# A four-layer graph network on one core: scores from the values' product, row vectors turned on VectorE, and graph attention's loops in step with the attention's half slots

## The chip, the cores and the metric

The kernel runs on one core of a Trainium2 chip. The core has TensorE (PE, matrix products, with weight loads shown apart as PEld), VectorE (DVE), ScalarE (ACT), GpSimd (POOL) and SyncE (SP), whose queue issues nearly all transfers here. The metric is the device time of one launch in microseconds; less is better. The time of the kernel before the change is 4863.75 us, the median of three runs (4861.99 to 4867.91).

## What is computed

Eight samples (B = 8) of N = 2048 nodes with 128 features pass through four layers, each as `x = x + layer(relu(layernorm(x)), adj)`. One 0/1 matrix `adj` (2048 x 2048, symmetric, with its diagonal) is shared. Everything is f32.

```python
def layer0(x):                       # graph attention with a normalised projection
    x = x * node_weights + node_bias + x
    h = layernorm(x @ W) * ln_gamma + ln_beta
    e = leaky_relu((h @ a1)[:, :, None] + (h @ a2)[:, None, :], 0.2)
    p = softmax(where(adj > 0, e, NEG_INF))
    return elu(p @ h + h)

def layer1(x):                       # four heads of 32, masked dot-product attention
    q, k, v = heads(x @ W_q), heads(x @ W_k), heads(x @ W_v)
    p = softmax(where(adj == 0, -inf, q @ k.T / sqrt(32)))
    return merge(p @ v) @ W_o + b_o

def layer2(x):                       # mean over the neighbours
    return relu(x @ W_self + b_self + (mask @ x / deg) @ W_neigh + b_neigh)

def layer3(x):                       # graph attention
    h = x @ W3.T
    e = leaky_relu((h @ a_src)[:, :, None] + (h @ a_dst)[:, None, :], 0.2)
    return softmax(where(adj == 0, -1e9, e)) @ h
```

## The kernel before

**The main stream.** Layer 1's attention is the longest part and is the frame for all else. It is cut into 8 x 8 x 4 = 256 blocks: sample, 256 rows of queries, head. A block has 12 positions (`SUB`), six for each half of 128 rows. In a half, position 0 issues the scores on PE (`scores`, L876) and the exponentials of the half before on ACT (L900); positions 0 and 1 also issue products of an earlier block's values (L927); position 2 masks the scores on DVE (L892); positions 3 and 4 transpose an earlier block's exponentials on PE (L912); positions 4 and 5 copy the transposed tiles to SBUF on ACT (`eT`, L917). A sample has 32 blocks, 384 positions.

**The side stream.** While the attention of sample b runs, the side work is layer 2 and layer 3 of sample b-1, layer 0 of sample b+1 and the projections for its attention, and the first part of layer 0 for sample b+2. It is written as a list of steps (`Steps`), each a few functions with a weight. `merged` lays two lists beside each other by weight. `work` then spreads the functions evenly over the positions of the window by their weights. The order of PE, DVE, ACT and POOL is the order in which this code issues instructions; each of these engines takes its instructions in that order. SP's order comes from the scheduler.

**Graph attention's loop** (`gat_loop`), used by layers 0 and 3. The 16 tiles of rows form six groups of 3, 3, 3, 3, 2, 2. For a group, the loop goes over 8 pairs of column tiles, and each pair passes through stages that lie one step apart:

- `leaky` (L464, ACT): leaky ReLU of the row scores along the free axis (`ab`, first half) plus a column score as bias;
- `lowered` (L470, DVE): minus the row's maximum (`ab`, second half);
- `exps` (L474, ACT), then `masked` (L479, DVE);
- `product` (L490, PE): 2 x n products into `gacc`; then `ended` and `closed`, which divide and add to x.

After the 8 pairs comes one step that starts no pair (`+ [None]`). Beside the pairs of one group, the steps of `ahead` prepare the next: the masks' load (`mg`), the maxima over a row's neighbours (`gat_maximum`, L404, DVE, with a load of `pmg`; in layer 0 all 16 are done before the loop), then `shifts` and `spread` in the fourth and fifth steps.

**Row vectors.** `spread` and `gat_rows` need vectors that lie along partitions turned along the free axis and copied to all partitions. `along_free` does it: a transpose on PE into PSUM (`prow`, L360), a copy on DVE put off by `later` (L364), a write to a small DRAM tile (`rowd`, L366), and a read that broadcasts it (`ab` or `s2b`, L367).

**Scores.** Layer 0 multiplies by W (L352), copies the result to `haug` (L561), normalises it (stats, root, apply, then gamma and beta on POOL, L567 and L570), turns it on PE again (`turned2`, copied by ACT as `h0nT`, L342) and multiplies the turned chunk with the two halves of `a` (`gat_scores`, L383). Layer 3 multiplies the turned chunk twice: with W3 transposed (L352) and with `wa3`, which is W3 transposed times the halves of `a` (L383). DVE copies the results to `s1` and `s2` and scales `s2n` (L386 to L388).

**PSUM.** The main and the side stream share three buffers of two banks (`ps2`). `later` keeps a read of such a buffer back until the next step or until a buffer is needed (`settle`, `psum`).

Of the kernel before, what the change touches and what calls it, by code (L numbers as in the profile page):

```python
# [18 lines left out]
P = 128  # L19
# [12 lines left out]
def gnn_kernel(  # L32
# [143 lines left out]
    nc.gpsimd.memset(neg_half, -0.5)  # L176

# [10 lines left out]
    w0 = load_w("w0", W0)  # L188
# [16 lines left out]
    NR = 2 * T + 4  # L205
# [4 lines left out]
    nc.scalar.dma_start(out=rows[2 * T + 2 : NR], in_=a3.rearrange("(c f) o -> c (f o)", c=2))  # L210
# [8 lines left out]
    a12_3 = cols[:, 2 * T + 2 : NR]  # L219
    w3T = const.tile([P, P], F32, name="w3T")  # L220
    pw3 = psum("pw3", (P, P))
    nc.tensor.transpose(pw3, w3, ident)
    nc.vector.tensor_copy(w3T, pw3)

    wa3 = const.tile([P, 2], F32, name="wa3")
    pwa = psum("pwa", (P, 2))
    nc.tensor.matmul(pwa, w3, a12_3, start=True, stop=True)
    nc.vector.tensor_copy(wa3, pwa)
# [12 lines left out]


# [44 lines left out]
    def norm_stages(src, dst, relu=False):  # L287
# [44 lines left out]

        return [stats, root, shift, apply_relu] if relu else [stats, root, apply]
# [14 lines left out]
    def rows_times(srcT, w, name):  # L348

        pt = psum(name)  # L350
        for k in range(4):
            nc.tensor.matmul(pt[:, k, :], srcT[:, k * P : (k + 1) * P], w, start=True, stop=True)  # L352
        return pt

    def along_free(col, dst):


        n = col.shape[1]
        pt = psum("prow", (n, P))
        nc.tensor.transpose(pt, col, ident)  # L360

        def read():
            row = small("row", (T, P))[0:n, :]
            nc.vector.tensor_copy(row, pt)  # L364
            d = new(dr2, "rowd", "rowd", (T, P))
            nc.sync.dma_start(out=d[0:n, :], in_=row)  # L366
            nc.sync.dma_start(  # L367
                out=dst, in_=d[0:n, :].rearrange("t p -> (t p)").partition_broadcast(P)
            )

        later(read)


    def gat_scores(st, g, hT, a12):

        if g == 0:
            st["s1"] = small("s1", (P, T))
            st["s2"] = small("s2", (P, T))
            st["s2n"] = small("s2n", (P, T))
        c = slice(4 * g, 4 * g + 4)  # L380
        pc = psum("psc", (P, 4, 2))
        for k in range(4):
            nc.tensor.matmul(pc[:, k, :], hT[:, k * P : (k + 1) * P], a12, start=True, stop=True)  # L383

        def read():
            nc.vector.tensor_copy(st["s1"][:, c], pc[:, :, 0])  # L386
            nc.vector.tensor_copy(st["s2"][:, c], pc[:, :, 1])
            nc.vector.tensor_scalar(st["s2n"][:, c], st["s2"][:, c], -1.0 / UP, None, ALU.mult)  # L388

        later(read)  # L390

    def gat_rows(st):

        st["s2b"] = new(sp2, "s2b", "s2b", (P, N))
        along_free(st["s2n"], st["s2b"])
# [12 lines left out]
    def gat_loop(st, finish, maxima):  # L408
# [19 lines left out]

        def shifts(k):
# [4 lines left out]
            cab = small("cab", (P, 6))[:, 0 : 2 * n]  # L434
# [4 lines left out]
        def spread(k):  # L439
            n = GROUPS[k][1]  # L440
            t = new(abp, "ab", "ab", (P, 2 * n * P))
            along_free(gr[k]["cab"], t)
            gr[k]["s1"], gr[k]["m"] = t[:, 0 : n * P], t[:, n * P : 2 * n * P]

        def ahead(k):
            if k >= len(GROUPS):
                return []
            return [
                [lambda: fetch(k), lambda: maximum(k, 0)],
                [lambda: fetch_mask(k, 0), lambda: maximum(k, 1)],  # L450
                [lambda: maximum(k, 2)],
# [65 lines left out]
        for k in range(len(GROUPS)):  # L517
            items += [(k, jp) for jp in range(T // 2)] + [None]
        stages = [leaky, lowered, exps, masked, product, ended, closed]
        nxt = []  # L520
        for step in range(len(items) + len(stages) - 1):
# [7 lines left out]
            for s in reversed(range(len(stages))):  # L529
                if 0 <= step - s < len(items) and items[step - s]:  # L530
                    fns.append(lambda f=stages[s], a=items[step - s]: f(*a))
# [4 lines left out]
    def layer0_ahead(b):  # L536

        st, h, hT, h2T = {}, {}, {}, {}
# [17 lines left out]
        def project(g):  # L556
# [4 lines left out]
            later(lambda: nc.scalar.copy(st["haug"][:, 4 * g : 4 * g + 4, 0:P], pt))  # L561
# [10 lines left out]
        def turned2(g):  # L572
            h2T[g] = chunk("h0nT")
            turn(hv(g), h2T[g])
# [7 lines left out]
            + norm_stages(hv, hv)  # L582
            + [scale, shift, turned2, lambda g: gat_scores(st, g, h2T.pop(g), a12_0)],
# [11 lines left out]
    def layer0_loop(b, st, maxima=False):  # L595
# [21 lines left out]
        return gat_loop(st, finish, maxima)  # L617
# [3 lines left out]
    def before_attention(b):  # L621
# [19 lines left out]
        def project(g):  # L641
            pq = psum("pq", (P, 512))
            nc.tensor.matmul(pq, wq, hT[g], start=True, stop=True)

            def read_q():
                qs = chunk("qs")
                nc.scalar.activation(qs, pq, AF.Copy, scale=-1.0 / (math.sqrt(HD) * UP))
                nc.sync.dma_start(out=qd[g], in_=qs)

            later(read_q)  # L650
            pk = psum("pk", (P, 512))
            nc.tensor.matmul(pk, wk, hT[g], start=True, stop=True)

            def read_k():
                kc = chunk("kc")
                nc.scalar.copy(kc, pk)
                nc.sync.dma_start(out=kd[g], in_=kc)

            later(read_k)
# [131 lines left out]
    def layer3(b):  # L791
# [13 lines left out]
        def project(g):  # L805
# [3 lines left out]
            pt = rows_times(hT[g], w3T, "ph3")  # L809
            later(lambda: nc.scalar.copy(st["haug"][:, 4 * g : 4 * g + 4, 0:P], pt))  # L810
# [5 lines left out]
            + [turned, project, lambda g: gat_scores(st, g, hT.pop(g), wa3)],  # L816
            1.0,
        )
        pre.add(1.0, lambda: gat_rows(st))
# [16 lines left out]
        return pre, gat_loop(st, finish, True)  # L836
# [245 lines left out]
    def mask_steps():  # L1082
# [35 lines left out]
        def degrees():  # L1118
# [10 lines left out]
            row = small("row", (T, P))  # L1129
# [32 lines left out]
    with tc.manual_schedule(engines=ENGINES):  # L1162
# [17 lines left out]
        LAG = 2 * SUB + 14  # L1180
# [26 lines left out]

        sts = {}
        for b in range(B):
            side = Steps()  # L1210
            if b >= 1:
                pre2, agg = layer2(b - 1)
                side.extend(pre2)
                pre3, loop3 = layer3(b - 1)
# [90 lines left out]
```

## Time and profile before

The profiled execution took 4871.3 us, and its span, from the first instruction to the last, is 4869.5 us. The page gives the busy time of each engine over the span, and groups of instructions with how often they ran, the busy time, the mean duration in ns, and the idle time of the engine just before them with what ended it. "out<-in" are the names of the tiles.

| what | value |
|---|---|
| median of three runs | 4863.75 us |
| profiled execution, its span | 4871.3 us, 4869.5 us |
| mean granted TensorE clock | 0.946 of full speed |
| ACT `eT` copies, L917 | 1024, busy 1018.4 us |
| ACT exponentials of the attention, L900 | 512, busy 1027.8 us |
| DVE masking of the attention, L892 | 1024, busy 1211.3 us |
| PE transposes of the attention, L912 | 8192 records, busy 1098.5 us |
| PE products of graph attention, L490 | 8192 records, busy 1114.1 us |
| ACT and DVE of graph attention, L464, L474, L470, L479 | 800.6, 591.5, 666.4, 662.0 us |
| DVE maxima, L404 | 256, busy 584.7 us |
| ACT `leaky` waiting for the transfer of `ab` | 96.3 us in 17 waits, the longest 22.3 |
| DVE waiting for `psc` (L386) | 90.4 us in 35 waits |

A row of the table is read so: the busy time is the sum of what the engine spent on the group, not of what the kernel would be shorter without it.

### The profile page before, as it was taken

How to read it: one execution, taken by the hardware profiler on the slowest of the kernel's cores; microseconds unless marked ns; L12 is line 12 of the kernel's file. 1: busy time of each engine (PE TensorE's matmuls, PEld its weight loads, DVE VectorE, ACT ScalarE, POOL GpSimd, SP SyncE). 2: the span in 40 equal slices, each digit the busy share in tenths (PEclk: the TensorE clock that was granted, in tenths of full speed). 3: DMA queues.
4: the chain of work that ended last, by engine and by line, in shares of the span. 5: the costliest groups of instructions: out<-in, count | busy, mean ns of one | idle time of the engine just before them, and what ended most of it. 6: DMA issues, size and time to landing. Idle time of an engine off the chain costs nothing.

```text
span 4869.5 us, 88275 instructions
## 1 busy us (share of the span) xinstructions
PE 4236.4 (87%) x34037; PEld 2898.0 (60%) x34037; DVE 3863.5 (79%) x8268; ACT 3643.9 (75%) x5153; POOL 437.4 (9%) x407
## 2 busy tenths in 40 slices
PE   3668998898998889898898988988899988999976
PEld 3545655565656666475665656566565656656645
DVE  5957776788978888788987889788887888758849
ACT  4637986697858888497885978588884888848926
POOL 2020002001200021001200012000210000000000
PEclk7868999999999999999999999999999999999988
DMA  8421123213231132312333132421324113222122
GB/s 269 135 88 54 47 61 97 92 49 102 81 126 57 57 107 79 124 50 76 91 105 95 57 94 85 122 65 55 107 76 130 48 58 98 79 86 62 47 92 75
DMA packets 303741, 423.37 MB, mean 87 GB/s; under 512 B 55844, under 2 KB 173016, under 8 KB 299224
## 3 DMA queue, kind: packets, MB, share of 16 engines
q1 hardware_dynamic: 301376, 416.84, 28.2%
q8 instruction: 269, 4.41, 0.4%
q14 instruction: 152, 1.25, 0.1%
q10 hardware_dynamic: 1944, 0.87, 0.1%
HBM read 365.77 MB, written 55.98 MB: 87 GB/s over the span
## 4 chain that ended last, share of the span: by engine, by line
PE 40%; DVE 31%; ACT 21%; issue 4%; DMA 4%; SPq 0%; POOL 0%; ACTq 0%; DVEq 0%; POOLq 0%
DVE e L892 9%; PE gacc L490 9%; PE pt L912 9%; ACT eT L917 6%; ACT e L900 6%; PE pagg L737 6%; PE sc L876 5%; DVE dump L404 5%; DVE ge L479 4%; DVE ge L470 4%; PE acc L927 4%; ACT ge L464 4%; ACT ge L474 2%; DVE ln_s L297 1%; DMA ab<-rowd 1%
## 5 line engine op out<-in xcount | busy, mean ns | idle before, releaser
L917 ACT COPY eT<-pt 128x1024 f32<-128x1024 f32 x1024 | 1018.4, 1011 | 666.4 <-PE pt L912 663.2
L892 DVE CUSTOM_DVE_ANT_0 e<-sc,pm 128x1024 f32<-128x1024 f32 x1024 | 1211.3, 1220 | 214.7 <-PE sc L876 205.6
L912 PE MATMUL pt<-ident,e 128*128 128x128 f32 x8192 | 1098.5, 282 | 187.0 <-DVE amh L892 106.0
L490 PE MATMUL gacc<-haug,ge 128*128 128x129 f32 x8192 | 1114.1, 286 | 123.4 <-DVE ge L479 121.2
L490 PEld LDWEIGHTS gacc<-haug,ge 128*128 128x128 f32 x8192 | 1011.9, 198 | 264.4 <-issue 134.7
L912 PEld LDWEIGHTS pt<-ident,e 128*128 128x128 f32 x8192 | 940.2, 145 | 341.4 <-DVE amh L892 137.4
L900 ACT ACTIVATE e<-e,amn 128x2048 f32<-128x2048 f32 x512 | 1027.8, 2007 | 20.9 <-DVE amn L896 20.8
L464 ACT ACTIVATE ge<-ab,s 128x384 f32<-128x384 f32 (+1 forms) x1536 | 800.6, 574 | 96.6 <-DMA ab<-rowd 96.3
L876 PE MATMUL sc<-ks,qr 32*128 32x512 f32 x4096 | 765.2, 668 | 55.8 <-ACT eT L917 40.5
L470 DVE TENSOR_TENSOR ge<-ge,ab 128x768 f32<-128x768 f32 (+1 forms) x768 | 666.4, 869 | 112.5 <-ACT ge L464 107.6
L479 DVE SCALAR_TENSOR_TENSOR ge<-mg,ge 128x768 f32<-128x768 fp8e4 (+1 forms) x768 | 662.0, 863 | 87.3 <-ACT ge L474 85.2
L474 ACT ACTIVATE ge<-ge 128x768 f32<-128x768 f32 (+1 forms) x768 | 591.5, 772 | 78.4 <-DVE ge L470 75.0
L927 PE MATMUL acc<-eT,vv 128*32 128x256 f32 x8192 | 612.5, 400 | 3.9 <-ACT eT L917 3.8
L404 DVE CUSTOM_DVE_ANT_0 dump<-s2b,pmg 128x2048 bf16<-128x2048 f32 x256 | 584.7, 2284 | 28.4 <-DMA s2b<-rowd 23.8
L307 POOL TENSOR_TENSOR ln_r<-ln_ve,neg_half 128x4 f32<-128x4 f32 x160 | 224.9, 1405 | 3872.8 <-DVE ln_ve L301 3781.0
L927 PEld LDWEIGHTS acc<-eT,vv 128*32 128x32 f32 x8192 | 196.6, 111 | 509.1 <-issue 430.2
L876 PEld LDWEIGHTS sc<-ks,qr 32*128 32x128 f32 x4096 | 231.9, 190 | 230.7 <-ACT eT L917 120.5
L737 PE MATMUL pagg<-mt,hm 128*128 128x512 fp8e4 x1536 | 356.7, 381 | 7.9 <-DVE agT L755 7.9
L737 PEld LDWEIGHTS <-hm 128*128 128x128 bf16 x1536 | 147.2, 98 | 182.0 <-issue 30.2
L339 PE MATMUL ptr<-ident,h 128*128 128x128 f32 x512 | 93.1, 308 | 46.1 <-DVE h L314 16.6
L980 DVE TENSOR_TENSOR aoT<-po,rT 128x256 f32<-128x256 f32 x64 | 27.1, 424 | 125.0 <-ACT rT L975 125.0
L339 PEld LDWEIGHTS ptr<-ident,h 128*128 128x128 f32 x512 | 65.5, 154 | 87.2 <-issue 26.6
(120 smaller groups left out, 2779.4 us busy)
## 6 DMA issues: line engine op xcount, KB each, us to landing
pmg<-pm_all SPq DMA_DIRECT2D x256, 256.0 KB
mg<-mg_all SPq DMA_DIRECT2D x128, 384.0 KB
pm<-pm_all SPq DMA_DIRECT2D x128, 256.0 KB
qr<-qd SPq DMA_DIRECT2D x1024, 32.0 KB
mt<-mt_all SPq DMA_DIRECT2D x64, 512.0 KB
ab<-rowd SPq DMA_DIRECT2D x64, 384.0 KB
adj<-in_adj_dram SPq DMA_DIRECT2D x16, 1024.0 KB
s2b<-rowd SPq DMA_DIRECT2D x16, 1024.0 KB
```

The costliest lines, as they stand in the source:

```text
L404: nc.vector.tensor_tensor_reduce(dump, st["s2b"], pm, UP, HIGHEST, ALU.add, ALU.min, st["mn"][:, it : it + 1])
L464: nc.scalar.activation(e[:, c, :], gr[k]["s1"], AF.Prelu, bias=st["s2"][:, j : j + 1], alpha=ALPHA)
L470: nc.vector.tensor_tensor(e, e, bc_mid(gr[k]["m"], 2), ALU.subtract)
L479: nc.vector.scalar_tensor_tensor(e, mt, BIG, e, ALU.mult, ALU.min)
L490: nc.tensor.matmul(gr[k]["acc"][:, q, :], e[:, c, q * P : (q + 1) * P], st["haug"][:, j, :], start=(j == 0 and q == 0), stop=(j == T - 1), ...
L737: nc.tensor.matmul(st["pa"], st["hm"][:, j, s, :], st["mt", g, j // 8][:, j % 8, :], start=(j == 0 and s == 0), stop=(j == T - 1 and s == ...
L876: nc.tensor.matmul(blk["sc"][g // 2][:, (g % 2) * 512 : (g % 2 + 1) * 512], blk["q"][r, t * P : (t + 1) * P], ks_t[b, hh][r, :], start=Tru ...
L892: nc.vector.tensor_tensor_reduce(e[:, c], blk["sc"][h], pm[:, c], UP, HIGHEST, ALU.add, ALU.min, mh[:, h : h + 1])
L900: nc.scalar.activation(blk["e"][t], blk["e"][t], AF.Exp, scale=-1.0, bias=blk["mn"][:, t : t + 1], accum_out=blk["ao"]["sum"][:, t, blk["h ...
L912: nc.tensor.transpose(pt[:, c, t, :], blk["e"][t][:, j * P : (j + 1) * P], ident)
L917: nc.scalar.copy(eT, blk.pop(("pt", w)).rearrange("p c t n -> p c (t n)"))
L927: nc.tensor.matmul(pair["acc"][g * HD : (g + 1) * HD, blk["hh"] % 2, :], vv_t[blk["b"], blk["hh"]][:, j, :], blk["eT"][w][:, g, :], start= ...
```

## The change

**Scores as further columns.** `w0` and `w3T` become 130 columns wide. The last two columns of `w3T` hold W3 transposed times the halves of `a`; those of `w0` hold W times gamma times the halves of `a`. `rows_times` then gives, beside the 128 values, the two scores of each node in the same products. In layer 0 they belong to the values before normalisation, so `gat_scores` corrects them with the mean, the inverse deviation and two sums per half (`gab`), in five small DVE instructions after a copy out of PSUM (`zs`). The second turn, its ACT copy and the products of `gat_scores` go. Layer 0's `score` stage stands after the root of the variance and before `apply`.

**Row vectors on DVE.** `along_free` turns with `nc.vector.transpose`, in 32 x 32 blocks. The vectors lie in zeroed tiles of 32 columns (`cabs`, three in turn; `s2ns`, two). The turned row then lies in four pieces on four groups of partitions, so four transfers write it to DRAM, and one broadcasts it as before. The transpose and its transfers are issued at once, not put off.

**q and k** of a chunk share one PSUM tile (`pqk`), read by one put-off function.

**Loops in step.** For samples 1 to 6, `work` now covers only layer 2, the maxima of layer 0 and the first five steps of layer 0's loop, in 63 positions. Then `locked` issues one loop step for every three positions (half of the six positions of a half of a block): each function of the step stands behind the first, second or third of them as `PLACES` (positions 0 to 2 of a half) or `PLACES_B` (positions 3 to 5) say. The steps of layer 3's preparation, or of the attention's preparation, are spread over the loop's first 0.7 or 0.6. In these windows the step without a pair after each group goes (`gap` is 0), and the five opening steps of layer 3's loop lie beside the last steps of layer 0's loop. `LAG`, by which the side stream ends after the window, is 36 positions and was 38.

```diff
     def rows_times(srcT, w, name):
-        pt = psum(name)
+        n = w.shape[1]
+        pt = psum(name, (P, 4, P if n == P else 2 * P))
         for k in range(4):
-            nc.tensor.matmul(pt[:, k, :], srcT[:, k * P : (k + 1) * P], w, start=True, stop=True)
+            nc.tensor.matmul(pt[:, k, 0:n], srcT[:, k * P : (k + 1) * P], w, start=True, stop=True)
         return pt
 
-    def along_free(col, dst):
-        n = col.shape[1]
-        pt = psum("prow", (n, P))
-        nc.tensor.transpose(pt, col, ident)
-        def read():
-            row = small("row", (T, P))[0:n, :]
-            nc.vector.tensor_copy(row, pt)
-            d = new(dr2, "rowd", "rowd", (T, P))
-            nc.sync.dma_start(out=d[0:n, :], in_=row)
+    def along_free(col, dst, n):
+        row = small("row", (P, 32))
+        nc.vector.transpose(row, col)
+        d = new(dr2, "rowd", "rowd", (T, P))
+        for g in range(4):
             nc.sync.dma_start(
-                out=dst, in_=d[0:n, :].rearrange("t p -> (t p)").partition_broadcast(P)
+                out=d[0:n, g * 32 : (g + 1) * 32], in_=row[g * 32 : g * 32 + n, :]
             )
-        later(read)
+        nc.sync.dma_start(
+            out=dst, in_=d[0:n, :].rearrange("t p -> (t p)").partition_broadcast(P)
+        )
 
-    def gat_scores(st, g, hT, a12):
+    def gat_scores(st, g, src, mean=None, r=None):
...
-        pc = psum("psc", (P, 4, 2))
-        for k in range(4):
-            nc.tensor.matmul(pc[:, k, :], hT[:, k * P : (k + 1) * P], a12, start=True, stop=True)
-        def read():
-            nc.vector.tensor_copy(st["s1"][:, c], pc[:, :, 0])
-            nc.vector.tensor_copy(st["s2"][:, c], pc[:, :, 1])
-            nc.vector.tensor_scalar(st["s2n"][:, c], st["s2"][:, c], -1.0 / UP, None, ALU.mult)
-        later(read)
+        s = st["s"][:, 4 * g : 4 * g + 4, :]
+        if mean is None:
+            nc.vector.tensor_copy(s, src)
+        else:
+            for c in range(2):
+                nc.vector.scalar_tensor_tensor(
+                    src[:, :, c], mean, gab[:, c : c + 1], src[:, :, c], ALU.mult, ALU.subtract
+                )
+            nc.vector.tensor_tensor(src, src, bc_last(r, 2), ALU.mult)
+            nc.vector.scalar_tensor_tensor(
+                s, src, -1.0, bc_mid(gab[:, 2:4], 4), ALU.mult, ALU.add
+            )
+        nc.vector.tensor_scalar(
+            st["s2n"][:, 4 * g : 4 * g + 4], s[:, :, 1], -1.0 / UP, None, ALU.mult
+        )
...
-            items += [(k, jp) for jp in range(T // 2)] + [None]
+            items += [(k, jp) for jp in range(T // 2)] + [None] * gap
...
+        PLACES = {'product': 1, 'masked': 0, 'exps': 1, 'lowered': 0, 'leaky': 1, 'ended': 1, 'closed': 0, 'maxi': 0, 'other': 2}
+        PLACES_B = {'product': 1, 'masked': 0, 'exps': 0, 'lowered': 1, 'leaky': 0, 'ended': 1, 'closed': 1, 'maxi': 1, 'other': 2}
+
+        def locked(loop, other, share):
+            k = 0
+            for n, (_, fns) in enumerate(loop):
+                cell = [[], [], []]
+                pl = PLACES_B if pos[0] % 6 >= 3 else PLACES
+                for f in fns:
+                    cell[pl[getattr(f, "place", "other")]].append((f, False))
+                want = min(len(other), math.ceil(len(other) * (n + 1) / (len(loop) * share)))
+                parts = []
+                while k < want:
+                    parts += [(f, i == 0) for i, f in enumerate(other[k][1])]
+                    k += 1
+                for i, p in enumerate(parts):
+                    cell[(i * 3) // len(parts)].append(p)
+                for c in cell:
+                    mains[pos[0]]()
+                    pos[0] += 1
+                    for f, first in c:
+                        if first:
+                            settle()
+                        f()
...
-                loop0 = layer0_loop(b + 1, sts[b + 1])
-                side.extend(merged(loop0, pre3, 0.85) if pre3 else loop0)
+                loop0 = layer0_loop(b + 1, sts[b + 1], gap=int(b == 0))
                 tail = before_attention(b + 1)
...
                 if loop3:
-                    side.extend(merged(loop3, tail, 0.7))
-                else:
-                    side.extend(tail)
+                    end = (b + 1) * per + LAG
+                    side.extend(loop0[:5])
+                    both = loop0[5:-6]
+                    both += [(0.0, u[1] + v[1]) for u, v in zip(loop0[-6:-1], loop3[:5])]
+                    both += [(0.0, loop0[-1][1] + loop3[5][1])] + loop3[6:]
+                    n = len(loop0) - 6
+                    work(side, end - 3 * len(both))
+                    locked(both[:n], pre3, 0.7)
+                    locked(both[n:], tail, 0.6)
+                    continue
+                side.extend(loop0)
+                side.extend(tail)
```

## The prediction

> **What bounds the kernel now.** I read the page's first part first, then the chain of waits, then the busy time of each engine by stretch.
>
> ```profile
> PE 4236.4 (87%) x34037; PEld 2898.0 (60%) x34037; DVE 3863.5 (79%) x8268; ACT 3643.9 (75%) x5153; POOL 437.4 (9%) x407
> PE 40%; DVE 31%; ACT 21%; issue 4%; DMA 4%; SPq 0%; POOL 0%; ACTq 0%; DVEq 0%; POOLq 0%
> ```
>
> PE is busiest, yet the chain changes engines all the time: three engines feed each other, and none is full. The share over the whole span hides the stages. The starts of the score products (L876) give them: 280 us of prologue, then eight sample windows (463, 586, 570, 571, 571, 568, 560 and 462 us), then a tail of some 230 us. Six windows are alike. One of them by stretch:
>
> ```profile
> core 0: us, PE busy (x) PEld busy (x) DVE busy (x) ACT busy (x) POOL busy (x), PEclk, DMA share, GB/s
> 1938.00:2052.00 114.00, 102.86 (x728) 56.84 (x726) 89.18 (x185) 49.70 (x58) 5.46 (x5) 0.99 0.45 141
> 2052.00:2250.00 198.00, 184.68 (x1613) 134.48 (x1614) 162.43 (x350) 183.25 (x266) 4.38 (x4) 0.98 0.18 52
> 2250.00:2278.00 28.00, 18.84 (x144) 9.71 (x142) 24.46 (x80) 12.47 (x15) 7.34 (x5) 0.82 0.17 53
> 2278.00:2509.00 231.00, 209.91 (x1736) 151.03 (x1737) 199.13 (x414) 202.48 (x301) 42.79 (x37) 0.96 0.31 91
> ```
>
> The rows are: aggregation and layer 0's maxima; layer 0's loop; the seam, where that loop drains and layer 3's starts; layer 3's loop with the next sample's preparation. PE is busy 516 of 571 us, 90.4%. It has 93% in the first loop, 67% in the seam, 91% in the second loop. In the two loops ACT has 93% and 88%, DVE 82% and 86%. So PE leads, ACT is level with it, and DVE is close in layer 3. Taking work off PE alone pays only while the other two follow. The best-filled long stretch shows what this code reaches:
>
> ```profile
> 2060.00:2240.00 180.00, 170.21 (x1504) 123.03 (x1500) 153.56 (x330) 168.66 (x248) 3.37 (x3) 1.00 0.18 53
> ```
>
> That is 94.6% for PE. I take it as the ceiling.
>
> **Part 1: scores as columns of the values' products, row vectors on DVE.** These groups go:
>
> ```profile
> L383 PE MATMUL psc<-cols,h0nT 128*128 128x2 f32 x256 | 37.4, 268 | 6.6 <-ACT h0nT L342 6.5
> L383 PE MATMUL psc<-wa,h3T 128*128 128x2 f32 x256 | 33.9, 254 | 0.2 <-ACT haug L810 0.2
> L339 PE MATMUL ptr<-ident,haug 128*128 128x128 f32 x128 | 23.4, 313 | 5.3 <-DVE s L387 2.8 <-POOL haug L570 1.0 <-DVE x L990 0.6
> L342 ACT ACTIVATE h0nT<-ptr 128x512 f32<-128x512 f32 x32 | 19.0, 595 | 35.8 <-PE ptr L339 35.7
> L360 PE MATMUL prow<-ident,cab 128*6 128x128 f32 (+1 forms) x96 | 28.4, 296 | 34.6 <-DVE cab L436 27.3 <-DVE amh L892 7.3
> ```
>
> With the 16 `prow` of `s2n` (4.5 us), PE loses 37.4 + 33.9 + 23.4 + 28.4 + 4.5 = 127.6 us, 16 us a sample. The wider products (130 columns for 128, on 43.1 + 38.9 us) return 1.3 us in all. Small products overlap their neighbours, so I count 15 us a sample. ACT loses 19 us, 2.4 a sample. The PSUM tiles of the side work also fall, from 82 to 52 a sample (no `prow` 14, `psc` 8, second turn 4; `pq` and `pk` share one). Each was a place where PE could wait for a reader; I give it no time of its own.
>
> DVE: the layer-0 score step has six small instructions instead of three. At the rows' 151 to 231 ns each this is 1.06 us for 0.51: +17.6 us over 32 chunks. Layer 3's has two for three: -0.15 us each, -4.8. The 112 row copies (273 ns) become 32x32-block transposes, which the trace does not show. Below them the smallest copies take 160 ns, above them is the 128-wide copy of 273 ns; I take 200, nearer the small ones as only 32 columns are read: -8 us. DVE nets +5 us in 3863, hidden at 80-odd% busy but exposed in layer 3's loop, where it would be 0.6 us a sample.
>
> SP: each row vector now takes four writes instead of one. That is 336 more issues at 263 ns (the median of the `rowd` write, L366), 88 us in all, 0.8 us of delay for each vector. Queued behind them on SP are the queries, mask rows and `pmg` loads; SP mostly waits for buffers, so they cost nothing while a vector is in time.
>
> **Part 2: loops in step with half slots.** In the six inner windows each step of a graph-attention loop now takes exactly three of the attention's positions. A window has 384 positions: 63 carry layer 2 and the maxima (the trace shows 65 today: 5.4 blocks of 12), and 321 carry 107 loop steps. So density stays what it was: 26.75 blocks beside the loops, about 26.5 now. What changes is evenness. The pause step after each group of rows goes (6 in each loop). The 5 opening steps of layer 3's loop lie beside the last steps of layer 0's, and so the 28 us seam at 67% should fill up. The two kinds of half slot get a fixed order: PE's scores and ACT's long exponential with DVE's masking in the first, PE's transposes and ACT's copies in the second; each loop stage needs only what an earlier step made.
>
> Demand in layer 3's loop while the preparation runs (8 steps, n=3, two attention blocks), from the groups' busy time in the window above over their counts: PE 13.0 for 96 products at 0.135, 18.6 for the blocks, 5 for the preparation, about 37 us; ACT 15.5, 16.2 and 5, the same; DVE 38 (16 large loop instructions at 0.95, four maskings at 2.5, three maxima at 2.27, some 6 for the preparation). Three engines within 4% of each other are hard to keep full, so I do not grant that loop the ceiling. PE's busy time in a window becomes 516 - 15 = 501 us. I take a fill of 92%, between today's 90.4% and the ceiling: 501 / 0.92 = 545 us, 26 less than 571. Six windows: -156.
>
> Outside them: the first window sheds two layer-0 preparations' scores and turns (17 us of PE at 88% busy), of which I count 12; the last window and the tail shed layer 3's scores and rows (6); the prologue is held by the adjacency's load and DVE, 3. Sum -156 - 21 = -177. The profiled execution took 4871.3 us (span 4869.5): 4694. The median of the runs stands 7.5 lower: 4687. I say **4690**.
>
> **The added wait, and a rule against it.** The row vector `ab` is now read sooner. `spread` stands in the third part of step 5 of a group; the next group's first `leaky` comes two to two and a third steps later. At about 4.1 us a step that is 8.2 to 9.5 us. Today row copy to first `leaky` is 13 to 15 us in layer 0's loop, and nothing waits there after a loop's first group. The vector needs: transpose 0.2, three extra issues 0.8, the write's landing 1.2 (row end to the broadcast's issue today), issue 0.35, broadcast 3.4 (chain of waits: 3.43 and 3.21): 5.9 us. It is in time by over 2 us. Behind a late one stand ACT's exponentials and the attention's `eT` copies, so PE too.
>
> The Trainium skill (DMA: Bandwidth & Descriptors, Specifications) says that transfers under 512 B are off line rate because the DMA engine reads, modifies and writes. The rows go from 512 B to 128 B pieces. By the trace's row the write lands as before; by the rule a read from HBM comes on top, for which the page's table of latencies gives 0.2 us on average and 2 us under load. Then the vector takes 6.1 to 7.9 us, still inside 8.2, with nothing left for a lagging DVE. I sum with the row and keep the rule for the slow case.
>
> **Rivals.**
> - *Work removed, fill unchanged.* For it: loop 1 already has 93%, layer 3's three engines are level, so order cannot give much. 501 / 0.904 = 554, -17 a window; -102 - 21: 4748, less 7.5: about 4740.
> - *The ceiling everywhere.* For it: one long stretch has it, and the granted clock is 1.00 there but 0.82 in the seam, so filled gaps also quicken PE. Against it: DVE's demand. 501 / 0.945 = 530, -41; -246 - 21: 4597.
> - *Slower: late row vectors.* Where: at the 12 group starts of each inner window, with no pause step left as slack. If DVE lags a step and a half when the transpose is due, the vector is some 6 us late, ACT stops and PE with it. 72 starts x 6 = 432 us, of which half may be made up in the attention's work: +216 on 4690, about 4905. It outweighs the gain from a mean net stall of 177 / 72 = 2.5 us. Against it: the slack above, and DVE is the lighter engine in layer 0's loop.
> - *No change.* The fixed order makes the fill worse and eats the removed work: 501 / 571 = 87.7%.
>
> **How the numbers follow.** Chances: forecast 0.42, fill unchanged 0.28, ceiling 0.16, no change 0.04, late vectors 0.10. A difference of 0.2% (10 us) is about what a measurement can tell from none. The first three are faster: 0.86; same 0.04; slower 0.10. The range takes the ceiling at its end and the unchanged fill with half of its gain lost: 4600 to 4800.
>
> **What would show it.** No `psc`, `h0nT` or `prow` rows; PE's busy time near 4110; inner windows of about 545 us with PE at 92%, without a stretch under 80% at the seam; group starts 33 us apart in layer 0's loop for 34 today. I am wrong if `ge<-ab` on ACT waits for the DMA of `ab` at group starts beyond the first, if `e` (L892's work) waits longer behind the maxima, or if the windows stay near 570 us with PE's busy time lowered.

## The result, and the profile after

The changed kernel takes 4787.78 us, the median of four runs (4782.57 to 4792.70); the kernel before, beside it, 4865.83. The ratio is 0.9836 (95% interval 0.9821 to 0.9852): 78 us faster, where 174 were forecast. The profiled execution has a span of 4790.8 us.

The first part of the page of the kernel after, and its chain of waits:

```profile
PE 4126.7 (86%) x33290; PEld 2842.0 (59%) x33290; DVE 3906.3 (82%) x8337; ACT 3613.4 (75%) x5121; POOL 454.9 (9%) x413
...
PE 33%; DVE 29%; ACT 28%; issue 6%; DMA 3%; SPq 1%; ACTq 0%; DVEq 0%
```

PE gave up 110 us of busy time, ACT 30. DVE, which was to gain 5, gained 43. In the chain PE's share fell by 7 points, and ACT's and the issue share rose by 9. PE bounds less than before, and the span fell by less than PE's busy time did.

The samples' windows, from one start of the score products to the next, in us:

| | first | 1 | 2 | 3 | 4 | 5 | 6 | last |
|---|---|---|---|---|---|---|---|---|
| before | 463.5 | 586.0 | 569.6 | 571.7 | 570.1 | 568.3 | 560.3 | 462.2 |
| after | 465.1 | 573.5 | 558.6 | 559.9 | 561.1 | 558.4 | 534.3 | 461.5 |

Window 6 fell by 26.0 us, the forecast for every inner window. It is also the only inner window without a next layer 0 whose preparation runs beside layer 3's loop. The other five fell by 9 to 12.5 us. So the missing time has a place. One of the five by stretch, in the busy time of each engine; first the kernel before: layer 0's loop from its first `leaky` to its last, the seam up to the next first `leaky`, layer 3's loop, and for comparison window 6.

```profile
core 0: us, PE busy (x) PEld busy (x) DVE busy (x) ACT busy (x) POOL busy (x), PEclk, DMA share, GB/s
2052.00:2243.00 191.00, 177.68 (x1547) 129.12 (x1548) 158.15 (x343) 177.38 (x259) 4.38 (x4) 0.98 0.18 51
2243.00:2277.00 34.00, 25.84 (x209) 15.08 (x207) 27.77 (x81) 17.86 (x21) 6.34 (x5) 0.85 0.20 61
2277.00:2498.00 221.00, 198.91 (x1630) 142.96 (x1631) 191.89 (x405) 193.36 (x290) 43.79 (x37) 0.95 0.31 92
3610.00:4170.00 560.00, 512.55 (x4129) 343.36 (x4125) 459.77 (x922) 435.95 (x611) 24.88 (x17) 0.96 0.28 84
```

The same view of the kernel after, with the whole window to which the three stretches belong ahead of window 6:

```profile
2024.00:2210.00 186.00, 174.04 (x1518) 127.29 (x1519) 159.45 (x344) 177.53 (x260) 4.37 (x4) 0.98 0.18 54
2210.00:2231.00 21.00, 18.21 (x165) 11.90 (x164) 19.11 (x46) 14.34 (x19) 1.01 (x1) 1.00 0.29 88
2231.00:2456.00 225.00, 189.40 (x1560) 138.63 (x1560) 205.94 (x447) 188.03 (x283) 52.28 (x40) 0.95 0.31 90
1876.00:2436.00 560.00, 500.97 (x4131) 346.75 (x4130) 483.37 (x1036) 444.29 (x636) 63.14 (x50) 0.97 0.29 87
3556.00:4090.00 534.00, 490.39 (x4080) 338.03 (x4078) 457.12 (x919) 433.37 (x611) 24.25 (x17) 0.98 0.30 88
```

The seam shrank from 34 to 21 us, and PE's share there rose from 76 to 87%. Layer 0's loop is 5 us shorter, with ACT now at 95% and PE at 94%. Layer 3's loop is 4 us **longer**, although PE has 9.5 us less to do in it: DVE went from 192 of 221 us (87%) to 206 of 225 (92%), and PE fell to 84%. The rest of the window, aggregation and maxima, grew from 124 to 128 us because it now holds 28 of the attention's maskings for 26; PE's share there rose from 91 to 93%. Over the whole window PE's busy time is 501 us, as forecast, but its fill is 89.5% and not 92%.

What filled DVE stands in its groups (count, busy us, mean ns, idle time before); first the score groups of the kernel before:

```profile
L388 DVE TENSOR_SCALAR s2n<-s 128x4 f32<-128x4 f32 x64 | 12.9, 202 | 2.2
...
L386 DVE COPY s<-psc 128x4 f32<-128x4 f32 x64 | 10.1, 158 | 90.5 <-PE psc L383 90.4
...
L387 DVE COPY s<-psc 128x4 f32<-128x4 f32 x64 | 9.7, 151 | 0.0
```

Then those of the kernel after:

```profile
L514 DVE TENSOR_TENSOR ge<-ge,ab 128x768 f32<-128x768 f32 (+1 forms) x768 | 683.8, 890 | 52.5 <-ACT ge L508 46.2 <-PE gacc L534 0.4
...
L429 DVE TENSOR_SCALAR s2n<-s 128x4 f32<-128x4 f32 x64 | 23.0, 360 | 2.2
...
L422 DVE SCALAR_TENSOR_TENSOR ln_z<-ln_mv,gab,ln_z 128x4 f32<-128x4 f32 x64 | 21.2, 372 | 0.0
...
L400 DVE STREAM_TRANSPOSE row<-cab 128x32 f32<-128x32 f32 x96 | 19.8, 206 | 0.3
...
L425 DVE TENSOR_TENSOR ln_z<-ln_z,ln_r 128x8 f32<-128x8 f32 x32 | 18.5, 579 | 3.3
...
L426 DVE SCALAR_TENSOR_TENSOR s<-ln_z,gab 128x8 f32<-128x8 f32 x32 | 5.3, 167 | 1.1
```

L422 to L429 are the score step, L400 the new turn, L514 the loop's `lowered`. With the two copies out of PSUM (L610 and L419, 5.3 us each) the scores cost 78.6 us of DVE. Before, the three groups of L386 to L388 cost 32.7. That is +45.9 us, where the prediction had 17.6 - 4.8 = +12.8. The turns went as expected: 206 ns for a guess of 200. `lowered`, which the change doesn't touch, took 17 us more (666.4 before); smaller changes elsewhere on DVE take about as much off again.

Means of 360, 372 and 579 ns beside 167 ns for as small an instruction hide two kinds of instance. The timeline of the kernel after (start, duration, engine, line) shows both:

```profile
2359.31 0.17 DVE L425 TENSOR_TENSOR ln_z<-ln_z,ln_r 128x8 f32<-128x8 f32 x1
...
2373.66 1.18 POOL L618 TENSOR_TENSOR haug<-haug,gam 128x512 f32<-128x512 f32 x1 [5.94 <-DVE haug L353]
...
2373.89 0.97 DVE L425 TENSOR_TENSOR ln_z<-ln_z,ln_r 128x8 f32<-128x8 f32 x1
2374.90 0.17 DVE L426 SCALAR_TENSOR_TENSOR s<-ln_z,gab 128x8 f32<-128x8 f32 x1
2374.92 1.19 POOL L621 TENSOR_TENSOR haug<-haug,bet 128x512 f32<-128x512 f32 x1
2375.10 1.04 DVE L429 TENSOR_SCALAR s2n<-s 128x4 f32<-128x4 f32 x1
```

The same multiplication takes 0.17 us alone and 0.97 when it starts during L618 on POOL: it ends when L618 ends. The next, L426, is short again: it starts 0.02 us ahead of L621. L429 starts during L621 and is held until that is done. Over the execution 16 of the 32 instances of L425 start during L618 or L621 and take 0.97 to 1.16 us; the other 16 take 0.17. The Trainium skill gives a reason (SBUF — State Buffer, SBUF: two separate sides): VectorE and GpSimd share a pair of ports, and where a VectorE instruction has two inputs in SBUF (or runs in a mode that takes both port pairs) and a GpSimd instruction that reads SBUF got the pair first, VectorE's stands still until the other ends. L425 and L422 have two such inputs and agree with it; L429 has one, was held all the same, and no run here shows in which mode it ran. The price is the row's, not the page's. The same hold reached `lowered`: 20 of its instances took 1.9 to 2.0 us, beside L621 or L694 on POOL; in the kernel before 5 took over 1.05. POOL's instructions are those of before but for six that set tiles once; it is the score step that now stands on DVE beside POOL's long instructions of the same preparation.

### The profile page after: what moved, and what is told of

Read it like the earlier page. It is cut to its first block, busy times and chain, and to the rows that moved or that the text cites. A ratio compares the mean times of both kernels' runs of the same rounds, so it can differ in the third digit from the quotient of the medians.

```text
span 4790.8 us, 87729 instructions
## 1 busy us (share of the span) xinstructions
PE 4126.7 (86%) x33290; PEld 2842.0 (59%) x33290; DVE 3906.3 (82%) x8337; ACT 3613.4 (75%) x5121; POOL 454.9 (9%) x413
## 4 chain that ended last, share of the span: by engine, by line
PE 33%; DVE 29%; ACT 28%; issue 6%; DMA 3%; SPq 1%; ACTq 0%; DVEq 0%
ACT e L956 8%; ACT eT L973 8%; PE pt L968 7%; DVE e L948 7%; PE pagg L787 7%; PE gacc L534 6%; ACT ge L508 6%; PE sc L932 5%; DVE dump L445 4%; DVE ge L514 4%; DVE ge L523 4%; PE acc L983 3%; ACT ge L518 3%; PE ph L393 1%; DVE ln_s L336 1%
## 5 line engine op out<-in xcount | busy, mean ns | idle before, releaser
L973 ACT COPY eT<-pt 128x1024 f32<-128x1024 f32 x1024 | 1007.3, 1012 | 568.7 <-PE pt L968 566.0
L968 PE MATMUL pt<-ident,e 128*128 128x128 f32 x8192 | 1079.0, 282 | 159.0 <-DVE amh L948 74.1
L932 PE MATMUL sc<-ks,qr 32*128 32x512 f32 x4096 | 786.9, 660 | 71.5 <-ACT eT L973 46.2
L514 DVE TENSOR_TENSOR ge<-ge,ab 128x768 f32<-128x768 f32 (+1 forms) x768 | 683.8, 890 | 52.5 <-ACT ge L508 46.2
L983 PE MATMUL acc<-eT,vv 128*32 128x256 f32 x8192 | 587.6, 397 | 2.6 <-ACT eT L973 2.6
L346 POOL TENSOR_TENSOR ln_r<-ln_ve,neg_half 128x4 f32<-128x4 f32 x160 | 207.2, 1295 | 3868.4 <-DVE ln_ve L340 3623.7
L983 PEld LDWEIGHTS acc<-eT,vv 128*32 128x32 f32 x8192 | 206.8, 111 | 508.7 <-issue 428.0
L932 PEld LDWEIGHTS sc<-ks,qr 32*128 32x128 f32 x4096 | 241.6, 189 | 263.9 <-ACT eT L973 142.5
```

Of the source, the lines that this page charges most:

```text
L514: nc.vector.tensor_tensor(e, e, bc_mid(gr[k]["m"], 2), ALU.subtract)
L932: nc.tensor.matmul(blk["sc"][g // 2][:, (g % 2) * 512 : (g % 2 + 1) * 512], blk["q"][r, t * P : (t + 1) * P], ks_t[b, hh][r, :], start=Tru ...
L968: nc.tensor.transpose(pt[:, c, t, :], blk["e"][t][:, j * P : (j + 1) * P], ident)
L973: nc.scalar.copy(eT, blk.pop(("pt", w)).rearrange("p c t n -> p c (t n)"))
L983: nc.tensor.matmul(pair["acc"][g * HD : (g + 1) * HD, blk["hh"] % 2, :], vv_t[blk["b"], blk["hh"]][:, j, :], blk["eT"][w][:, g, :], start= ...
```

## The experiments

Thirteen kernels ran. My theory after the result was that **DVE in layer 3's loop** ate the gain; the rivals were that PE now waits for its one accumulator since the pause step is gone, that the placing of the preparation is at fault, and that the removed PE work was never worth much. Ratios are against the kernel before, run beside each (medians 4865 to 4868 us); where a difference is to another kernel, the text names it.

**Part 1 alone.** Scores, turns and the shared `pqk` as after, in the loops of before. Diffs are against the kernel after unless another is named.

```diff
-        LAG = 2 * SUB + 12
+        LAG = 2 * SUB + 14
-                pre3, loop3 = layer3(b - 1, int(b + 1 == B))
+                pre3, loop3 = layer3(b - 1)
-                    locked(both[:n], pre3, 0.7)
-                    locked(both[n:], tail, 0.6)
+                    side.extend(merged(loop3, tail, 0.7))
```

> The scores as columns, the turns on VectorE and the shared q/k tile alone, with the loops spread by weight as before the change. Theory A (VectorE has become the limit where layer 3's loop meets the next sample's preparation, so PE work taken off pays little): 4840 to 4870 us, PE busy about 4125, inner windows within 5 us of 570. Rival B (the gain of 78 us is the removed PE work, the step order is worth nothing): 4780 to 4800. Rival C (the removed work is worth its 121 us of PE and the step order loses some of it again): 4740 to 4755.

It took 4883.16 us, ratio 1.0037 (1.0025 to 1.0049): part 1 alone makes the kernel **slower**, with 85 us less of PE and 29 more of DVE. That lies outside all three ranges that were expected.

**The steps alone.** Old scores and PE's turns, whose copies DVE now issues at once (a diff against the kernel before, with `locked` and its tables as in the change).

```diff
-        later(read)
+        read()
-                    side.extend(merged(loop3, tail, 0.7))
+                    locked(both[:n], pre3, 0.7)
+                    locked(both[n:], tail, 0.6)
```

> The loops in step alone, with the scores by products of their own and the row vectors turned on PE as before (the row's copy follows its transpose at once instead of being put off). Theory A: 4795 to 4825 us, so most of the 78 us, with PE busy back at about 4236 and the seam between the loops filled. Rival B: within 15 us of 4864. Rival C: slower than 4864 by 20 us or more.

4860.74 us, ratio 0.9993 (0.9987 to 1.0000). The seam is as short as after the change (about 20 us), yet nothing is gained: layer 3's loop grew from 221 to about 230 us and the stretch ahead of layer 0's loop from 124 to 130. Waits of this kernel in 230 us around that loop (sum, times, longest):

```profile
DVE row L368 <- PE prow L364: 9.9, 4, 4.4
```

DVE, the engine that is short there, stands for the turn on PE. A turn on DVE has no such wait. But in the kernel before, whose copies are put off, the same wait was 8.5 us over the whole execution; the steps with copies put off were not run, so this kernel doesn't price the step order with PE's turns at its best.

**The accumulator.** With no pause step, one group's products wait until DVE has read the last group's sums. Waits of the kernel after in the window 1876 to 2436:

```profile
PE gacc L534 <- DVE x L881: 10.4, 4, 5.7
...
ACT ge L508 <- DMA ab<-rowd: 6.9, 3, 4.0
PE gacc L534 <- DVE hp L658: 4.6, 4, 2.3
```

The experiment issues `ended` one position earlier (in `PLACES_B` too).

```diff
-        PLACES = {'product': 1, 'masked': 0, 'exps': 1, 'lowered': 0, 'leaky': 1, 'ended': 1, 'closed': 0, 'maxi': 0, 'other': 2}
+        PLACES = {'product': 1, 'masked': 0, 'exps': 1, 'lowered': 0, 'leaky': 1, 'ended': 0, 'closed': 0, 'maxi': 0, 'other': 2}
```

> The changed kernel with the reciprocal and the closing additions of a group issued behind the first position of a half slot, ahead of masked and lowered on VectorE, in place of behind the second. The trace shows PE's first product of a group waiting for these (about 15 us in an inner window). If that wait sets the end (theory A in part): 4740 to 4765 us and the waits of gacc for the lines 881 and 658 under 4 us a window. If VectorE is the limit and the wait only shows it: 4780 to 4795.

The waits fell as wanted:

```profile
PE gacc L534 <- DVE x L881: 2.4, 1, 2.4
...
PE gacc L534 <- DVE hp L658: 2.0, 2, 1.4
```

The time rose to 4821.17 us, ratio 0.9908 (0.9893 to 0.9922), 33 above the kernel after; layer 0's loop went from 186 to 190.5 us. Ten us of waits taken from PE in a window made the window longer, presumably since DVE's division now stands ahead of the masking that ACT and PE wait for. In that loop PE's wait of the scores for the `eT` copies rose from 3.8 to 7.7 us; the cause was not traced further. So shortening the wait for the accumulator in this way does not bring the gain.

**Less work for DVE.** The maxima inside the loops, and those of the first sample ahead of them, 144 in all, go over 1024 columns only; that half of the maximum is left out.

```diff
-                gat_maximum(st, i0 + q)
+                gat_maximum(st, i0 + q, N if st.get("full") else N // 2)
```

> The changed kernel with layer 3's maxima taken over the first 1024 of the 2048 columns: 1.1 us less VectorE time for each of 128, 18 us a sample in layer 3's loop and the tail, nothing else changed. Theory A: 4690 to 4720 us (inner windows 10 us shorter or more, the tail some 15). Rivals B and C, in which PE is the limit: 4765 to 4780, the tail alone.

4682.28 us, ratio 0.9628 (0.9609 to 0.9646): 153 us less of DVE brought 106 us. By windows, 71 us of it lie in the six inner ones, some 18 in the tail and 11 in the prologue. Layer 3's loop in the windows view:

```profile
2189.00:2405.00 216.00, 189.63 (x1557) 136.84 (x1556) 191.45 (x447) 187.46 (x283) 46.12 (x40) 0.94 0.31 94
```

PE has the same 189 us there as after the change; DVE has 14.5 less, and the stretch is 9 shorter. So DVE's work holds it, though not one for one.

**The preparation spread** over 0.95 of layer 3's loop instead of 0.6.

```diff
-                    locked(both[n:], tail, 0.6)
+                    locked(both[n:], tail, 0.95 if b < B - 2 else 0.6)
```

> The changed kernel with the next sample's preparation spread over 0.95 of layer 3's loop in place of 0.6 (windows 1 to 5). Theory A2: VectorE's demand then is even over the loop, 4735 to 4770 us. If the loop is limited by waits within a step and not by the sum of work: within 10 us of 4788.

4791.00 us, ratio 0.9842 (0.9826 to 0.9859): no change. DVE's work in the loop fell by about 6 us, the loop by 1 at most. So DVE's sum within the loop is not all.

**The correction once a sample.** Layer 0's correction for 16 tiles at once: 5 instructions for 20 of a sample.

```diff
         def score(g):
-            mv, r = norm2[0].st[g]
-            gat_scores(st, g, zs.pop(g), mv[:, :, 0], r)
+            if g == G - 1:
+                gat_scores(st, 0, kept("z"), kept("mv")[:, :, 0], kept("r"), T)
```

> The changed kernel with layer 0's correction of the scores done once for all 16 tiles after the fourth chunk, five instructions a sample in place of twenty. In the trace a score instruction that overlaps GpSimd took about 1 us for 0.17, some 5.5 us a sample beyond the bare durations. Theory A2 (VectorE limits layer 3's loop with the preparation): 4745 to 4775 us, VectorE's busy time down by 30 to 45 us. If VectorE is not the limit there: 4783 to 4792.

4767.08 us, ratio 0.9793 (0.9778 to 0.9808): 21 below the kernel after, for 31 us less of DVE. The same added to part 1 in the loops of before:

> Columns, turns and shared q/k tile in the old loops (4883 in the first round), with layer 0's score correction done once for 16 tiles. Theory A2 (the columns cost 39 us against the turns alone because five small dependent VectorE instructions, stretched beside GpSimd, stand ahead of the loop's own work four times a sample): 4850 to 4865. Rival F (the loss lies elsewhere: the shared q/k tile, which holds one of three PSUM buffers through two copies, or the shifted weights of the spread): 4873 to 4885.

4852.86 us, ratio 0.9970 (0.9959 to 0.9981): 30 below part 1 alone.

**The correction on GpSimd.** The kernel with the correction once a sample, but POOL does it: DVE has none of the correction's small instructions left that could be held.

```diff
-                nc.vector.scalar_tensor_tensor(
-                    src[:, :, c], mean, gab[:, c : c + 1], src[:, :, c], ALU.mult, ALU.subtract
+                nc.gpsimd.tensor_scalar(
+                    t[:, :, c], mean, ngab[:, c : c + 1], zero1, ALU.mult, ALU.add
...
-            nc.vector.tensor_tensor(src, src, bc_last(r, 2), ALU.mult)
+            nc.gpsimd.tensor_tensor(src, src, t, ALU.add)
+            nc.gpsimd.tensor_tensor(src, src, bc_last(r, 2), ALU.mult)
+            nc.gpsimd.tensor_tensor(s, src, bc_mid(gab[:, 2:4], n), ALU.add)
```

> The changed kernel with the correction done once for 16 tiles and on GpSimd instead of VectorE. It takes the last five small instructions a sample off VectorE (12 us in all by their durations in the run with the scores done at once). Theory A2: 4750 to 4766 us. If GpSimd's own work stretches VectorE's loop instructions as much as is saved: 4765 to 4775.

**4743.46 us**, ratio 0.9746 (0.9724 to 0.9767), the fastest kernel with the whole computation. Page, then groups, then one window of it:

```profile
PE 4112.4 (87%) x33290; PEld 2829.9 (60%) x33290; DVE 3866.9 (82%) x8178; ACT 3612.9 (76%) x5121; POOL 481.6 (10%) x462
```

```profile
L435 POOL TENSOR_TENSOR kept_z<-kept_z,kept_r 128x32 f32<-128x32 f32 x8 | 6.0, 748 | 0.6
...
L437 DVE TENSOR_SCALAR s2n<-s 128x4 f32<-128x4 f32 x32 | 5.4, 170 | 1.1
```

```profile
1849.00:2403.00 554.00, 501.89 (x4128) 346.35 (x4127) 477.82 (x1014) 444.03 (x635) 67.60 (x56) 0.97 0.29 88
```

DVE's busy time is 3.4 us above the kernel before, nearly the +5 of the prediction, and `s2n` on DVE, now layer 3's alone (L437), takes 170 ns, where the mean over both layers was 360. Fill is 90.6%. Against the kernel with the correction once on DVE the time fell by 24 us. DVE's busy time fell by 8 only: some 20 us of correction left it, and some 15 came back in layer 0's normalisation (L361, from 42.6 to 50.1 us) and in `lowered`, of which more instances now stand beside POOL.

With the preparation spread over 0.8 on top of that:

```diff
-                    locked(both[n:], tail, 0.6)
+                    locked(both[n:], tail, 0.8 if b < B - 2 else 0.6)
```

> As the run with the scores on GpSimd, with the preparation spread over 0.8 of layer 3's loop in windows 1 to 5. The spread over 0.95 took 6 us of VectorE busy time off layer 3's loop and 1 us off its length. Expected: within 8 us of the run with the scores on GpSimd; 10 us or more below it if evenness was held back by the score step.

4764.49 us, ratio 0.9791 (0.9773 to 0.9808): 21 slower than with 0.6. I expected no such loss and cannot explain it; layer 3's loop went from 217 to 222 us although DVE's busy time fell by 10 us over the span.

**Turns, steps and columns apart.** Four more kernels fill the table: the turns on DVE in the kernel before; the same with the shared `pqk`; steps and turns with the old scores; and the columns with the correction on POOL in the loops of before. Their core edits are those shown above or in the change:

```diff
-        pt = psum("prow", (n, P))
-        nc.tensor.transpose(pt, col, ident)
+        row = small("row", (P, 32))
+        nc.vector.transpose(row, col)
```

> The kernel before with only the row vectors turned on VectorE and written in four pieces. Theory A2: 4850 to 4870 us, near no change, so that the 18 us which columns, turns and shared tile cost together in the old loops lie with the columns. Rival E (the four small writes and the earlier issue cost): 4878 to 4890, waits for ab or s2b longer.

4844.09 us, ratio 0.9950 (0.9935 to 0.9965).

> The turns alone (4844) with the shared q/k tile added, in the old loops. Theory A2: 4838 to 4850, no change. Rival F: 4860 or more.

4839.89 us, ratio 0.9945 (0.9929 to 0.9962): the shared tile does no harm.

> The changed kernel with the scores made as before the change (second turn of layer 0's values, products of their own), so loops in step and row vectors on VectorE without the columns. The first round left 4861 for the steps alone, where VectorE's copy of a row stood waiting for PE's transpose (10 us of a window's layer 3 loop). Theory A2 (the turn on VectorE is what the step order needed, and the columns' relief of PE is eaten by the longer score step on VectorE): 4775 to 4805 us. Rival D (PE's relief by the columns is what the step order needed): 4840 to 4865.

4814.67 us, ratio 0.9891 (0.9875 to 0.9908).

> Columns, turns and shared tile in the old loops, with the score correction once for 16 tiles and on GpSimd, so that the columns' relief of PE and ACT stands there without their cost on VectorE. In the order by steps the same relief took the time from 4815 to 4743 us (72 of 95 us of PE work). Theory A3 (the relief pays only in the order by steps, as in the old loops PE waits for its partners and not for its own work): 4830 to 4850, at most 10 us below the 4840 without columns. Rival G (the relief pays in either order once VectorE is free of the correction): 4770 to 4800.

4835.77 us, ratio 0.9945 (0.9925 to 0.9965).

All with the turns on DVE and the shared tile, medians in us:

| | old scores | columns, correction on DVE | columns, correction once a sample, on POOL |
|---|---|---|---|
| loops of before | 4840 | 4883 | 4836 |
| loops in step | 4815 | 4788 | 4743 |

Read along the rows: the columns take 88 us of PE's busy time away in the loops of before (4216.1 to 4128.2) and 98 in step (4210.8 to 4112.4). In the loops of before that is worth 4 us, in step 71. The correction on DVE costs 47 us in the one and 44 in the other against the last column, which differs in two things: doing it once a sample gives 30 and 21 of these, the move to POOL 17 and 24. Read down: the step order is worth 25 us with the old scores, 95 with the columns as changed and 92 with the relieved PE. So what one edit is worth hangs on the other; the order with PE's turns, copied at once, gained nothing (4861 for 4865).

## Why the prediction was wrong, by its steps

- **What bounds.** "Taking work off PE alone pays only while the other two follow" held. I wrote it and then costed the window as if they would: in layer 3's loop DVE rose to 92%, and PE fell to 84%.
- **PE's work.** Right: 4127 busy for "near 4110", 501 us in an inner window.
- **DVE's sum. The step that failed:** "DVE nets +5 us in 3863, hidden at 80-odd% busy". It is +43, from the scores' +45.9 for +12.8. The rows I took (means of 151 to 231 ns) were of small instructions that read PSUM or seldom met POOL; the new ones read SBUF beside POOL's gamma and beta. The sign stood in one of these rows: L388's mean of 202 ns is 62 instances of 170 and two of 1180, and those two ran beside POOL's gamma and beta. Of the three that POOL stretches, the time above the bare duration is 13.2 us (L425), 12.1 (L429) and 10.1 (L422), 35.4 in all, about the whole error of 33. Nor was it hidden: the correction taken off DVE gave 44 us of the 98 between forecast and result. The prediction also put nothing for the loop's own instructions: `lowered` grew by 17 us. That comes with the step order, as it is there with the old scores too (684.7) and not with the columns in the loops of before (667.1).
- **The fill of 92%.** The second part, and the other 53 us. Even with DVE relieved, the mean inner window is 551.1 us for 571.0 before, so six brought 119 us and not 156 (-37); the first window brought 4 of 12 (-8); the rest is in smaller items and in the 7.5 us allowed from profile to median. The place is layer 3's loop again: in that kernel it lasts 217 us, PE is busy 87% of it and DVE 92%, where PE has 93% in layer 0's loop and in the stretch ahead of it. The prediction's own sum had the three engines within 4% of each other there; it granted the window 92% all the same. Fill is 90.6%, the figure of the rival "work removed, fill unchanged", which gave 4740: that kernel took 4743. That the numbers meet does not prove the rival: in the loops of before the same work was removed and the mean fill fell from 90.6 to 88.7%. Window 6 alone met the forecast, but there fill was 91.5% before and 91.8% after, and PE lost 22 us and not the counted 15: a forecast met by luck, with that rival's mechanism.
- **Seam.** Right in kind: 34 to 21 us, PE 87%. The steps alone had the same seam and gained nothing, as the other stretches gave it back.
- **Group starts.** Right in layer 0's loop: six starts at 2024.0, 2053.1, 2088.2, 2123.3, 2155.5 and 2184.2 are 29 to 35 us apart. In layer 3's loop they are 29 to 47.
- **Row vectors.** Right. One vector in the timeline of the kernel after, from the turn to the first `leaky` that needs it:

```profile
2046.32 0.20 DVE L400 STREAM_TRANSPOSE row<-cab 128x32 f32<-128x32 f32 x1
2046.55 1.27 SPq L403 DMA_DIRECT2D rowd<-row  x4
2048.81 0.34 SPq L406 DMA_DIRECT2D ab<-rowd  x1
...
2053.12 1.14 ACT L508 ACTIVATE ge<-ab,s 128x384 f32<-128x384 f32 x2
```

The broadcast's issue comes 2.3 us after the row's end (1.2 to 1.4 before), and `leaky` starts with no wait. The fourth write is issued 1.0 us after the first, for the 0.8 that was counted. The broadcast starts 1.08 us after the end of that issue (median of the execution), and 1.05 us after the end of the one write of 512-B rows before: the trace's row held, and the price that the rule of the Trainium skill (DMA: Bandwidth & Descriptors, Specifications) would add for 128-B pieces does not show. ACT's waits for `ab` in a window fell from 12.2 to 6.9 us; the rival of late vectors fell.
- **The pause steps.** I gave them no price. PE waits 15 us in a window for the accumulator instead; the one try that removed 10 of these lost 33 us, so their price is not known.

What stays open: why the relief of PE is worth nearly nothing in the loops of before, where layer 3's loop lasts 218 us with 190 of PE, for 219 with 197 without the columns, and in layer 0's loop, 190.7 us long in that kernel, neither PE nor ACT reaches 95%; that the pause steps and the uneven places set its length is argued, not shown. The 21 us of the spread on top of POOL's correction are open as well.

## What to carry to other kernels

Work taken off the busiest engine may be worth little where the second one is nearly full, so add up the second engine by stage, in the stage where both are near 90%, before granting a fill. A small instruction is priced by the row of one with the same operands and the same neighbours: here one with two inputs in SBUF that started behind a long GpSimd instruction cost that instruction's remainder. Look at the spread of a row too, not only at its mean. Where two edits are made together, run all four corners; here one gave 4 us or 71, by the order that the other had set.

## What the runs showed of the hardware

Three kinds of small VectorE instructions stood until a GpSimd instruction beside them ended, L618 or L621, each of 128x512 f32: 167 ns became 971 to 1160 (16 instances of L425), 170 became 1032 to 1041 (14 of L429), 215 became some 1.2 us (10 of the 64 of L422). Who is first seems to decide. L426 was never held in the kernel after, where it starts 20 ns ahead of L621. In the kernel with the correction once a sample the same operation (L430) was held in the four instances that GpSimd led by 6 ns or more, and not in the three that it led by 5 or less. The recorded start is not exact for that: nine of the ten held instances of L422 are shown 20 to 50 ns ahead of GpSimd's. Reads of PSUM were not held: in the kernel before, three copies (L386, L387) ran inside such GpSimd instructions in 148 to 161 ns. And not every GpSimd instruction holds: beside the root (L346, 1.3 us in the mean) one instance of L425 and two of L422 took their bare 166, 211 and 215 ns.

Moving work from VectorE to GpSimd paid although the two hold each other up: the correction once a sample took 23 us of POOL (its five groups' sum), in instructions of 0.25 to 0.75 us, and the time fell by 24 us, though VectorE's own instructions took back some 15 of the 20 us that it was spared. And a 32x32-block transpose of 128x32 f32 costs 206 ns.
